# Moving three kinds of work between the even and the odd tiles of a 200-tile attention loop: value roundings, key parts, and the steps of a key part

## The chip, the cores and the metric

One core of one Trainium2 chip. The metric is device microseconds (us) of one execution of the whole program. Of the kernel before there are three timed runs and one execution that the hardware profiler recorded.

## What is computed

A layer norm, a cross attention with 16 heads of 32 channels, a residual, a second layer norm, a gated feed-forward block with quantised inputs and a second residual. 1600 query rows look at 5776 context rows. What the change touches lies in the attention: keys are quantised for each row and head, values for each channel over all rows.

```python
def _fq_sym(x, axis):
    s = jnp.max(jnp.abs(x), axis=axis, keepdims=True) / 127.0
    s = jnp.maximum(s, 1e-08)
    q = jnp.clip(jnp.round(x / s), -127.0, 127.0) * s
    return x + jax.lax.stop_gradient(q - x)
...
kv = (cond @ Wkv + bkv).reshape(1, -1, 2, H, hd)
k, v = (kv[:, :, 0], kv[:, :, 1])
...
q = _fq_sym(q, axis=-1)
k = _fq_sym(k, axis=-1)
v = _fq_sym(v, axis=2)
attn = jnp.einsum('bhqd,bhkd->bhqk', q, k)
attn = jax.nn.softmax(attn.astype(jnp.float32), axis=-1)
attn = _fq_unsigned(attn, axis=-1)
out = jnp.einsum('bhqk,bhkd->bhqd', attn, v)
```

## The kernel before

**Stages.** A prologue (up to about 140 us in the trace) makes the queries of all heads and the keys and values of heads 0 to 3. Then comes one loop of 200 tiles (140 to 1553 us), and last the feed-forward block.

**A tile** (the loop at L1231) is one head against one block of 128 query rows: 5776 scores for each row, made in five chunks. TensorE writes a chunk to PSUM (L1251; L1260 in a pair tile), and VectorE copies it to the buffer `score` while it takes the row maxima (L1267, called here an eviction). There are two score buffers, used in turn. GpSimd makes of the five maxima the bias of the exponential (L1299, then L1310 and L1311, the last called nb). ScalarE makes the exponentials as bytes in two halves (L1203): `pairc` at the end of the tile, `codes` in the tile after. SyncE issues a DMA transpose for each half (L1208, L1211), GpSimd unpacks the first half three tiles later (L1224), and TensorE multiplies with the values four tiles later (L1130).

**Groups.** Heads go in four groups of four, 50 tiles to a group. Tiles are numbered from 0 here, in the kernel 50 g + k; "tile 12" is k = 12 of a group, and even and odd are by that number. Two heads have 25 tiles: 13 for the first and 12 for the second, since tile 12 of the first is a pair tile: its 128 rows are the last 64 query rows of both heads, so it needs the keys of both.

**Side work.** While a group is scored, the keys and values of the next group are made, a pair of 126-row blocks in two tiles. TensorE projects (L276, L278) into one PSUM tile `pp` for each pair of blocks, of which there is a single buffer; ScalarE copies it out (`pair_keep`, L299, tile `vraw`) at the end of the odd tile, and only then TensorE goes on to the next pair in the even tile after. GpSimd rounds the keys (L316, L323, L324) in odd tiles.

**Key parts.** The keys of a head become a bf16 matrix kT in six parts. `keys_split` (L373) makes a sum of three bf16 pieces of a part on GpSimd: step 0 is L387 and L388, step 1 is L390 and L391, step 2 is L393. `keys_turn` (L395) transposes the pieces on TensorE (L400), `keys_keep` (L402) copies them to kT on ScalarE (L404). A pair (n, turn) in `PLAN["keys"]` or `LAST["keys"]` says: split from tile n on, turn and keep in tile `turn`. `plan_keys` (L730) puts steps 0 and 1 in tile n and step 2 in tile n + 1, or all three in tile n where turn is n + 1. The first of the four tuples is for the second head of the group itself; its last part is turned in tile 12.

**Values.** When all blocks of the next group are projected, `values_divide` (GpSimd, L360) and `values_round` (ScalarE, L363, to int8) go over the values in pieces that `PLAN["divide"]` lists, the first number being the tile, from tile 49 of one group to tile 15 of the next. They are planned by `plan_codes` (L747). Group 0 takes its own list, `CODES`, and the end of that of `PLAN["divide"]`; group 3 has a list of its own, `PLAN["end"]`. `values_copy` (L414, L419) makes the f16 values of one head in two halves, in the tiles that `PLAN["copy"]` names.

**Order.** Nothing is scheduled by a program: `put` (L727) adds a call to one of a tile's lists. In a tile, GpSimd does its list "pool", the unpacking, and then the maxima and nb. ScalarE does "act0" (kT copies) and `codes` of the tile before in the window that says "turn" in `WINDOWS` (L113), then "act" (the copy of `pp` first, then roundings), then its own `pairc`. Each engine takes its instructions in that order.

**Group 3** (`LAST`) makes no further keys and values. It runs the output projection instead (L790 to L807), with `part_turn` in every third tile from tile 8 on; if that tile turns no keys, four matmuls that are only there to keep TensorE busy (`keep_busy`, L817) are added.

Of the kernel before, what the change touches and what calls it, by code (L numbers as in the profile page):

```python
# [22 lines left out]
P = 128  # L23
C = 512
H = 16
HD = 32
# [3 lines left out]
NB = 46  # L30
# [18 lines left out]
MAXIMA = ((23, 0, 0, 24, 32), (35, 1, 24, 36, 64), (41, 2, 36, 42, 128))  # L49

CODES = (
    (1, 0, 4, 0, 128), (1, 4, 23, 0, 32), (1, 23, 46, 0, 32), (2, 4, 8, 32, 128), (3, 8, 24, 32, 64), (5, 24, 40, 32, 64),
)

PLAN = {

    "keys": (
        ((-4, 0), (2, 4), (4, 6), (6, 8), (8, 10), (10, 12)),
        ((12, 14), (14, 16), (16, 18), (18, 20), (20, 22), (22, 24)),
        ((24, 26), (26, 28), (28, 30), (30, 32), (32, 34), (34, 36)),  # L60
        ((36, 38), (38, 40), (40, 42), (42, 44), (44, 46), (48, 49)),
    ),
    "query": ((0, 4, 5), (14, 14, 18), (25, 27, 29), (39, 41, 43)),
    "copy": ((8, 10, 11), (19, 21, 23), (31, 33, 35), (50, 50, 51)),

    "max": (
        *((31 + i, 0, 0, 30, 16 * i, 16 * i + 16) for i in range(8)),
# [2 lines left out]
    "finish": (47, 48),  # L70

    "divide": (
        (49, 0, 23, 0, HD), (49, 23, NB, 0, HD), (50, 0, 4, HD, P), (51, 4, 8, HD, P), (51, 8, 24, HD, 2 * HD),
        (53, 24, 40, HD, 2 * HD), (55, 40, NB, HD, 2 * HD), (57, 8, 16, 2 * HD, P), (59, 16, 24, 2 * HD, P),
        (61, 24, 32, 2 * HD, P), (63, 32, 40, 2 * HD, P), (65, 40, NB, 2 * HD, P),
    ),
    "end": (
        (49, 0, 23, 0, HD), (49, 23, NB, 0, HD), (50, 0, 4, HD, P), (51, 4, 16, HD, P), (52, 16, 28, HD, P),
# [6 lines left out]

LAST = {
    "keys": (
        ((-4, 0), (4, 5), (6, 7), (8, 9), (10, 11), (11, 12)),
        tuple((n, n + 1) for n in range(12, 24, 2)),
        tuple((n, n + 1) for n in range(24, 36, 2)),  # L90
    ),
    "query": ((0, 4, 5), (14, 14, 18), (25, 27, 29)),
    "copy": ((8, 9, 10), (19, 21, 22), (31, 33, 34)),
# [52 lines left out]
def xattn_ffn(ctx: ExitStack, tc: tile.TileContext, xin, ctxt, wq, bq, wkv, bkv, wp, bp, w13, w2, nw, out):  # L146
# [340 lines left out]
    with (  # L487
# [165 lines left out]
        for t in range(NB):  # L653
# [11 lines left out]
            if t % 8 == 7 or t in (43, NB - 1):  # L665
                c0 = 44 if t == NB - 1 else t // 8 * 8
# [13 lines left out]
        for t in range(NT):  # L680
            n = WHEN["first"] + WHEN["every"] * t
# [13 lines left out]
        n = WHEN["first"] + WHEN["every"] * 7 + WHEN["store"] + 4  # L695
# [18 lines left out]
    with tc.manual_schedule():  # L714
# [12 lines left out]
        def put(n, where, fn, *args, first=False):  # L727
            plan[n][where].insert(0 if first else len(plan[n][where]), lambda: fn(*args))

        def plan_keys(h, n, turn, c0):  # L730
            if turn > n + 1:
                put(n, "pool", keys_split, h, c0, (0, 1))
                put(n + 1, "pool", keys_split, h, c0, (2,))
            else:
                put(n, "pool", keys_split, h, c0)
            put(turn, "turn", keys_turn, h, c0, psa)
            put(turn, "act0", keys_keep, h, c0)
# [282 lines left out]
        for g in range(H // G):  # L1020
            base = g * 50
            h = g * G
            own = LAST if g + 1 == H // G else PLAN
            for hx, starts in zip(range(h + 1, min(h + 5, H)), own["keys"]):
                for i, (n, turn) in enumerate(starts):
                    if base + n >= 0:
                        plan_keys(hx, base + n, base + turn, 8 * i)
            if g == 0:
                put(2, "act", query_load, h, 8 * P, NQ)

                for c, *fn in (
                    (0, warm_up, 5), (1, keys_turn, 0, 40, psa), (1, keys_keep, 0, 40), (1, values_max, 0, 3, 42, NB),
                    (2, values_turn, 0, 4, psa, "oacc"), (2, values_scale, 0), (2, values_diag, 0),
                    (2, keys_turn, 0, 44, psa), (2, keys_keep, 0, 44),
                    (4, values_spread, 0, psa, "oacc"), (4, values_keep, 0),
                ):
                    put(0, f"w{c}", *fn)
                for n in range(1, LAG):
                    for c in range(5):
                        put(n, f"w{c}", warm_up, 3 if c in (1, 3) else 1)  # L1040
                put(2, "w3", values_sum, 0, psa)
                put(2, "w3", values_sum_keep, 0, nc.scalar)
                put(2, "w4", values_rest, 0)
                put(3, "act0", values_rest_keep, 0, nc.scalar)
                for n, *args in (*CODES, *((n - 50, *args) for n, *args in PLAN["divide"] if n > 53)):
                    put(n, "pool", values_divide, 0, *args)
                    put(n, "act0" if args[0] == 0 else "act", values_round, 0, *args)
                put(2, "pool", values_copy, 0, 0)
                put(2, "pool", values_copy, 0, 1)
# [4 lines left out]
            if g + 1 == H // G:  # L1054
# [6 lines left out]
                for j in range(NT):  # L1061
                    n = base + LAST["first"] + 3 * j
# [13 lines left out]
                for k in range(8):  # L1076
                    n = base + LAST["piece"][k]
# [153 lines left out]
        for n in range(NTI):  # L1231
# [7 lines left out]
            h, t = tiles[n]  # L1239
# [190 lines left out]
```

## Time and profile before

| | |
|---|---|
| three timed runs | 1813.94, 1815.35, 1825.12 us; median 1815.35 us |
| the profiled execution | 1815.99 us |
| its span, first to last instruction | 1814.2 us |
| VectorE busy | 1692.9 us (93%) |
| TensorE matmul busy | 1624.5 us (90%) |
| ScalarE busy | 1485.2 us (82%) |
| GpSimd busy | 1322.3 us (73%) |
| TensorE clock granted, mean | 0.985 |

In the rows of the profile, engines are PE (TensorE), PEld (its weight loads), DVE (VectorE), ACT (ScalarE), POOL (GpSimd) and SP (SyncE); L360 is line 360 of the kernel before. A row of groups gives line, engine, operation, output<-input, shapes and count, then busy time and the mean of one, then the idle time before them and who ended it. A row of a timeline gives start and duration in us and, in brackets, the idle time before and who ended it.

### The profile page before, as it was taken

What the parts mean: (1) busy time and instruction counts of PE and PEld (TensorE: products, weight loads), DVE (VectorE), ACT (ScalarE), POOL (GpSimd) and SP (SyncE); (2) the same over time, 40 slices, a digit from 0 to 9 for tenths busy, and PEclk for the clock granted to TensorE, in tenths of its full rate; (3) what the DMA queues carried; (4) which work ended last, traced back from release to release, by engine and by line L of the source; (5) the groups of instructions that cost most, each with busy time, mean ns of one, the idle gap of its engine ahead of it and who ended that gap; (6) DMA issues with size and microseconds to landing.
All of it is one profiled execution on the core that took longest, in us unless ns stands there. A gap on an engine that the chain in (4) does not pass through costs nothing. (4 is left out here: it accounts for less than half of the span.)

```text
span 1814.2 us, 43710 instructions
## 1 busy us (share of the span) xinstructions
PE 1624.5 (90%) x16745; PEld 1139.5 (63%) x16745; DVE 1692.9 (93%) x2930; ACT 1485.2 (82%) x1471; POOL 1322.3 (73%) x1852
## 2 busy tenths in 40 slices
PE   7998989988898998888888988888998899889998
PEld 6985666656565665565566665655565555568886
DVE  7889999999999999999999999999899999788886
ACT  4557999988899998888999998998899988744443
POOL 5657989877899888788898887888777756542221
PEclk9999999999999999999999999999899999999999
DMA  5656999999999999999999999989999999821000
GB/s 169 158 146 131 208 209 204 207 202 212 189 208 204 210 209 207 206 210 194 199 204 205 208 221 207 201 157 201 196 215 208 211 210 238 185 81 36 30 27 21
DMA packets 982447, 323.87 MB, mean 179 GB/s; under 512 B 939943, under 2 KB 946267, under 8 KB 982238
## 3 DMA queue, kind: packets, MB, share of 16 engines
q1 hardware_dynamic: 970392, 300.91, 87.5%
q10 hardware_dynamic: 11846, 20.17, 3.9%
q8 instruction: 131, 2.15, 0.5%
q14 instruction: 78, 0.64, 0.1%
HBM read 79.16 MB, written 10.72 MB: 50 GB/s over the span
## 5 line engine op out<-in xcount | busy, mean ns | idle before, releaser
L1267 DVE TENSOR_SCALAR_CACHE_REDUCE score<-sl 128x1536 f32<-128x1536 f32 (+1 forms) x1000 | 1301.3, 1355 | 42.9 <-PE sl L1251 25.5
L1251 PE MATMUL sl<-kT,qT 96*128 96x512 bf16 (+1 forms) x2304 | 628.4, 367 | 117.3 <-DVE score L1267 107.4
L1203 ACT ACTIVATE pairc<-score,nb,qs 128x2772 uint8<-128x2772 f32 x192 | 518.4, 2700 | 73.2 <-POOL nb L1311 56.1
L1203 ACT ACTIVATE codes<-score,nb,qs 128x3024 uint8<-128x3024 f32 x192 | 558.2, 2907 | 19.3 <-DMA rT<-codes 18.0
L1224 POOL CAST rU<-pk 128x2816 f16<-128x2816 uint8 x200 | 506.4, 2532 | 6.5 <-DMA pk<-pairc 5.6
L276 PE MATMUL pp<-wkv,cb 128*128 128x256 f32 x1104 | 340.3, 389 | 22.4 <-ACT vraw L299 19.4
L1251 PEld LDWEIGHTS <-qT 96*128 96x128 bf16 x2304 | 184.0, 96 | 211.2 <-issue 140.7
L276 PEld LDWEIGHTS pp<-wkv,cb 128*128 128x128 f32 x1104 | 197.4, 190 | 122.4 <-ACT vraw L299 40.2
L1130 PEld LDWEIGHTS <-rT 128*128 128x128 f16 x4608 | 195.6, 96 | 94.9 <-issue 13.5
L1130 PE MATMUL oacc<-v,rT 128*128 128x32 f16 x4608 | 210.7, 177 | 4.8 <-ACT og L1169 3.5
L1310 POOL TENSOR_SCALAR m<-mx,m 128x1 f32<-128x1 f32 x200 | 72.5, 362 | 146.1 <-DVE score L1267 91.4
L1130 PEld LDWEIGHTS <-rU 128*128 128x128 f16 x4224 | 146.1, 96 | 42.6 <-issue 8.3
L1130 PE MATMUL oacc<-v,rU 128*128 128x32 f16 x4224 | 167.5, 177 | 0.0
L961 POOL TENSOR_TENSOR rw<-rl,nw_b 128x480 f32<-128x480 f32 (+3 forms) x39 | 49.1, 1260 | 151.4 <-DVE gq L991 63.6
L943 PE MATMUL p<-w13l,hT 128*128 128x480 f32 (+3 forms) x312 | 120.5, 386 | 3.8 <-POOL w13l L481 3.6
L943 PE MATMUL p<-w13h,hT 128*128 128x480 f32 (+3 forms) x312 | 122.3, 392 | 1.8 <-ACT hT L928 1.2
L404 ACT COPY kT<-kt 96x1008 bf16<-96x1008 bf16 (+2 forms) x97 | 90.7, 935 | 6.7 <-PE kt L400 6.5
L299 ACT COPY vraw<-pp 128x512 f32<-128x512 f32 x92 | 53.1, 578 | 45.9 <-DVE am L288 40.0
L1299 POOL TENSOR_SCALAR m<-mx 128x1 f32<-128x1 f32 x200 | 74.3, 372 | 18.2 <-DVE score L1267 18.1
L316 POOL TENSOR_TENSOR vraw<-vraw,rs 128x256 f32<-128x256 f32 x92 | 59.1, 643 | 35.8 <-DVE rs L311 22.8
L1267 DVE DVE_READ_ACCUMULATOR score<-sl 128x1 f32 x1000 | 83.3, 83 | 0.0
L943 PEld LDWEIGHTS p<-w13h,hT 128*128 128x128 f32 (+1 forms) x312 | 59.3, 190 | 16.9 <-ACT hT L928 7.0
(229 smaller groups left out, 2619.0 us busy)
## 6 DMA issues: line engine op xcount, KB each, us to landing
cb<-in SPq DMA_DIRECT2D x135, 256.0 KB
cr<-in SPq DMA_DIRECT2D x46, 256.0 KB
qT<-q_dram SPq DMA_DIRECT2D x45, 100.0 KB
pk<-pairc SPq DMA_TRANSPOSE x200
rT<-codes SPq DMA_TRANSPOSE x200
xn<-in ACTq DMA_DIRECT2D x12, 256.0 KB
x_s<-in ACTq DMA_DIRECT2D x12, 256.0 KB
x_dram<-x_s ACTq DMA_DIRECT2D x12, 256.0 KB
```

The lines of the kernel that those rows point to most:

```text
L276: nc.tensor.matmul(pp, cbs[g, t][:, kb, :], wts_g[g][:, kb, :], start=(kb == 0), stop=False)
L299: nc.scalar.copy(vraw.rearrange("p (u t) c -> p u t c", t=2)[:, u : k + 1 : k - u], pp.rearrange("p t (two c) -> p two t c", two=2),)
L316: nc.gpsimd.tensor_tensor(kv, kv, batch.pop(("rs", g, u)).unsqueeze(3).broadcast_to([P, 2, G, HD]), ALU.mult,)
L404: nc.scalar.copy(kT[h][:, c0 * KB : (c0 + n) * KB].rearrange("p (b k) -> p b k", k=KB), exp_.pop(("pt", h, c0))[:, :n, 2:])
L943: nc.tensor.matmul(pt[:r, :w], T["h", t][:, kb, :r], last_w[c][p][:, i * 4 + kb, :], start=(kb == 0 and p == 0), stop=(kb == 3 and p == 1),)
L1130: nc.tensor.matmul(oacc[h][:, t, :], turned(n, bl), v16[h][:, bl, :], start=(bl == turns[0]), stop=(bl == turns[-1]),)
L1203: nc.scalar.activation(dst, src, AF.Exp, bias=nb, scale=s1, accum_out=usum[:, i, n % 50 : n % 50 + 1])
L1224: nc.gpsimd.tensor_copy(r.rearrange("p (b two) q -> p b two q", two=2), packed.pop(n).bitcast(U8).rearrange("p b (q two) -> p b two q", tw ...
L1251: nc.tensor.matmul(sl[:, x0:x1], qT[h][:, t * P : (t + 1) * P], kT[h][:, col + x0 : col + x1], start=True, stop=True,)
L1267: nc.vector.tensor_scalar(sc[:, col : col + w], sl[:, :w], 1.0, None, ALU.mult, ALU.max, accum_out=mx[:, c : c + 1])
L1299: nc.gpsimd.tensor_scalar(m1, mx[:, 0:1], mx[:, 1:2], mx[:, 2:3], ALU.max, ALU.max)
L1310: nc.gpsimd.tensor_scalar(m2, mx[:, 3:4], mx[:, 4:5], m1, ALU.max, ALU.max)
```

## The change

The kernel's lists are edited, and one division of work.

- `plan_keys`: step 1 of a key part goes from tile n to tile n + 1, ahead of step 2, wherever the part is not turned in tile n + 1.
- `PLAN["divide"]`: all pieces from tile 51's second on move one tile later, so that from tile 52 to 66 they lie in even tiles, both the GpSimd division and the ScalarE rounding. `CODES` drops its last piece, and the filter for group 0 takes one entry more, so that the same pieces are done there one tile sooner or later than before.
- `PLAN["keys"]`, first tuple: parts two to six are split and turned two tiles sooner; the last turn is in tile 10. Group 0 keeps the old tiles (`FIRST_KEYS`).
- `PLAN["copy"]`: the two halves of the second head's values in tiles 7 and 9, not 8 and 10.
- `LAST["keys"]` (group 3): the second head's parts are turned in tiles 5, 6, 7, 9 and 10, not 5, 7, 9, 11 and 12; the parts of the third and fourth heads are placed at 0, 2, 3, 5, 6 and 8 tiles from tiles 12 and 24, not at every second tile. No key turn now shares a tile with a `part_turn`, so `keep_busy` adds its matmuls in five tiles more: 11, 17, 23, 29 and 35.

On VectorE and in SyncE's queue the order of instructions is the same; on GpSimd and ScalarE the same instructions stand in another order; TensorE gets 20 `keep_busy` matmuls more, and its key transposes stand elsewhere.

```diff
 CODES = (
-    (1, 0, 4, 0, 128), (1, 4, 23, 0, 32), (1, 23, 46, 0, 32), (2, 4, 8, 32, 128), (3, 8, 24, 32, 64), (5, 24, 40, 32, 64),
+    (1, 0, 4, 0, 128), (1, 4, 23, 0, 32), (1, 23, 46, 0, 32), (2, 4, 8, 32, 128), (3, 8, 24, 32, 64),
 )
+FIRST_KEYS = ((-4, 0), (2, 4), (4, 6), (6, 8), (8, 10), (10, 12))
...
     "keys": (
-        ((-4, 0), (2, 4), (4, 6), (6, 8), (8, 10), (10, 12)),
+        ((-4, 0), (1, 2), (2, 4), (4, 6), (6, 8), (8, 10)),
...
-    "copy": ((8, 10, 11), (19, 21, 23), (31, 33, 35), (50, 50, 51)),
+    "copy": ((7, 9, 11), (19, 21, 23), (31, 33, 35), (50, 50, 51)),
...
     "divide": (
-        (49, 0, 23, 0, HD), (49, 23, NB, 0, HD), (50, 0, 4, HD, P), (51, 4, 8, HD, P), (51, 8, 24, HD, 2 * HD),
-        (53, 24, 40, HD, 2 * HD), (55, 40, NB, HD, 2 * HD), (57, 8, 16, 2 * HD, P), (59, 16, 24, 2 * HD, P),
-        (61, 24, 32, 2 * HD, P), (63, 32, 40, 2 * HD, P), (65, 40, NB, 2 * HD, P),
+        (49, 0, 23, 0, HD), (49, 23, NB, 0, HD), (50, 0, 4, HD, P), (51, 4, 8, HD, P), (52, 8, 24, HD, 2 * HD),
+        (54, 24, 40, HD, 2 * HD), (56, 40, NB, HD, 2 * HD), (58, 8, 16, 2 * HD, P), (60, 16, 24, 2 * HD, P),
+        (62, 24, 32, 2 * HD, P), (64, 32, 40, 2 * HD, P), (66, 40, NB, 2 * HD, P),
     ),
...
 LAST = {
     "keys": (
-        ((-4, 0), (4, 5), (6, 7), (8, 9), (10, 11), (11, 12)),
-        tuple((n, n + 1) for n in range(12, 24, 2)),
-        tuple((n, n + 1) for n in range(24, 36, 2)),
+        ((-4, 0), (4, 5), (5, 6), (6, 7), (8, 9), (9, 10)),
+        *(tuple((n + i, n + i + 1) for i in (0, 2, 3, 5, 6, 8)) for n in (12, 24)),
     ),
...
             if turn > n + 1:
-                put(n, "pool", keys_split, h, c0, (0, 1))
-                put(n + 1, "pool", keys_split, h, c0, (2,))
+                put(n, "pool", keys_split, h, c0, (0,))
+                put(n + 1, "pool", keys_split, h, c0, (1, 2))
...
-                for i, (n, turn) in enumerate(starts):
+
+                for i, (n, turn) in enumerate(starts if g or hx > 1 else FIRST_KEYS):
...
-                for n, *args in (*CODES, *((n - 50, *args) for n, *args in PLAN["divide"] if n > 53)):
+                for n, *args in (*CODES, *((n - 50, *args) for n, *args in PLAN["divide"] if n > 52)):
```

## The prediction, on record before the changed kernel ran

> **What bounds the kernel now.** I read the page's engine shares first, then the costliest groups, then busy time by stretches of group 1, then the timeline of single tiles. The page:
>
> ```profile
> PE 1624.5 (90%) x16745; PEld 1139.5 (63%) x16745; DVE 1692.9 (93%) x2930; ACT 1485.2 (82%) x1471; POOL 1322.3 (73%) x1852
> ...
> L1267 DVE TENSOR_SCALAR_CACHE_REDUCE score<-sl 128x1536 f32<-128x1536 f32 (+1 forms) x1000 | 1301.3, 1355 | 42.9 <-PE sl L1251 25.5
> ```
>
> VectorE's evictions are the floor: only 42.9 us of idle time lie before them, so no reordering of side work can win more. Stretches of group 1 (us, then busy time of PE, PEld, DVE, ACT, POOL): two tiles without a stall, tiles 10 and 11, tile 12, tiles 18 to 33:
>
> ```profile
> 536.01:549.24 13.23, 12.15 (x146) 8.55 (x144) 13.23 (x23) 12.02 (x12) 12.19 (x19) 1.00 1.04 215
> ...
> 562.98:576.88 13.90, 12.77 (x158) 8.62 (x156) 13.37 (x23) 13.08 (x14) 12.86 (x20) 1.00 1.19 214
> 576.88:586.18 9.30, 7.37 (x83) 4.43 (x82) 6.84 (x13) 9.23 (x9) 8.40 (x13) 1.00 0.99 172
> ...
> 614.07:725.48 111.41, 100.24 (x1155) 68.22 (x1154) 108.66 (x181) 102.34 (x85) 95.27 (x145) 1.00 1.10 209
> ```
>
> A pair of tiles costs 13.23 when VectorE never waits; tile 12 costs 9.30 with 6.84 of VectorE work. Its stall in the timeline:
>
> ```profile
> 578.66 0.56 ACT L299 COPY vraw<-pp 128x512 f32<-128x512 f32 x1
> ...
> 580.94 1.76 DVE L1267 TENSOR_SCALAR_CACHE_REDUCE score<-sl 128x1536 f32<-128x1536 f32 x1 [1.15 <-PE sl L1260]
> ...
> 582.48 0.77 ACT L404 COPY kT<-kt 96x756 bf16<-96x756 bf16 x1
> ...
> 583.30 0.38 PE L1260 MATMUL sl<-kT,qT 96*64 96x512 bf16 x1 [0.82 <-ACT kT L404]
> 583.71 1.22 DVE L1267 TENSOR_SCALAR_CACHE_REDUCE score<-sl 128x1024 f32<-128x1024 f32 x1 [1.00 <-PE sl L1260]
> ```
>
> Two waits: 1.15 us because ScalarE copied `pp` late (TensorE may not project the next pair before, and the score matmuls queue behind that projection), and 1.00 us because the last key part reaches kT in the tile that uses it. Why the copy is late, on GpSimd:
>
> ```profile
> 552.71 0.67 POOL L390 TENSOR_TENSOR kd<-kd,stack 128x256 f32<-128x256 f32 x1
> 553.44 0.40 POOL L391 CAST stack<-kd 128x256 bf16<-128x256 f32 x1
> ...
> 558.36 0.26 POOL L1311 TENSOR_SCALAR nb<-m,nqs 128x1 f32<-128x1 f32 x1
> 558.70 1.27 POOL L360 TENSOR_TENSOR vraw<-vraw,tops 128x512 f32<-128x512 f32 x1
> 559.93 0.67 POOL L393 TENSOR_TENSOR stack<-kd,stack 128x256 bf16<-128x256 f32 x1
> ...
> 565.57 0.26 POOL L1311 TENSOR_SCALAR nb<-m,nqs 128x1 f32<-128x1 f32 x1
> ```
>
> GpSimd runs without a gap here. From one nb to the next an odd tile with a division takes 565.57 - 558.36 = 7.21, an even tile with steps 0 and 1 takes 6.42 (nb of tile 5 at 537.56, of tile 6 at 543.98). Last evictions end about 6.45 (odd) and 6.8 (even) after the ones before. So nb falls behind: it ends 0.90 after the last eviction where GpSimd keeps up, 2.07, 2.47, 3.11 and 3.14 after it in tiles 5, 7, 9 and 11. The exponentials wait for it, and the copy of `pp` behind `codes`. In tiles 7, 9 and 11 that copy ends 1.72, 1.82 and 2.34 into the next tile, and VectorE idles 0.42, 0.53 and 1.15; at 0.76 (tile 5) it doesn't. So it idles by what the copy ends beyond about 1.3.
>
> **The change part by part.**
>
> *Key part of tile 12, groups 1 and 2.* The wait of 1.00 goes in each: -2.0. The part is turned in tile 10; nothing reads it before tile 12. The five transposes, copies and splits that move two tiles sooner issue no DMA; SyncE's order is untouched. What is late next is the copy of `pp`, so no more than the 1.00 is counted.
>
> *Divisions and step 1 change places.* L390 and L391 take 1.23 with their gaps (525.30 to 526.53), the division of 128x512 also 1.23 (558.70 to 559.93). Where both exist, the GpSimd passes stay 6.42 and 7.21. But the second key part is now split whole in tile 1: the three steps take 2.77 busy (0.63, 0.40, 0.67, 0.40, 0.67), some 3.0 with gaps, and a division of 1.27 leaves for tile 2. So nb of tile 1 ends at about 0.9 + 1.3 = 2.2, not 0.91; the value copy (0.80) in tiles 7 and 9 makes these passes 8.0; tiles 10 and 11 shrink to some 5.3.
>
> *Roundings in even tiles.* On ScalarE, odd `pairc` to even `pairc` takes 6.48 now (524.09 to 530.57, with the kT copy), even to odd 6.1 and a rounding of 0.6. After: 7.1 and 6.1. Queued behind the rounding are the tile's own `pairc`, then `codes` and the copy of `pp`, for which TensorE waits; before, the rounding stood behind that copy. The copy ends 0.7 less into the next tile than the even `pairc` starts after its last eviction (tile 4: 1.46 and 0.76). Carried on from tile 1, `pairc` starts 2.1, 2.2, 2.9, 2.8 and 2.65 late in tiles 2, 4, 6, 8 and 10, stalls in between included. VectorE then idles 0.6, 0.2, 1.0, 0.8 and 1.0 in tiles 4, 6, 8, 10 and 12, and as before 0.67 in tile 2: 4.3. Before it was 0.67, 0.11, 0.42, 0.53 and, of tile 12, 1.46 without the kT wait: 3.2. So +1.1 each in groups 1 and 2: +2.2. Bounds: -1.5 if the fuller ScalarE only loses the gaps that it has now (0.83, 0.59 and 0.54 before `pairc` in tiles 5, 8 and 9), +4 if each of six roundings delays TensorE by its 0.61.
>
> *Group 0.* The kT wait stays. By the same steps (tile 3's pass grows by 1.23, tile 4's rounding comes before the copy) idle time goes from 3.7 to 4.3: +0.6, bounds -1 and +2.5.
>
> *Step 1 in odd tiles outside the divisions.* The odd pass grows from 7.21 - 1.23 = 5.98 to 7.21, the even one falls to 5.19. Odd nb ends at 0.9 + 7.21 - 6.45 = 1.7; the even pass makes that good. `pairc` of the even tile then starts 1.7 + 6.48 - 6.8 = 1.4 late, and the copy of `pp` ends at 0.7, inside the 1.3: nothing, covered by 0.6 us of slack. Tiles 19 and 21 also make value copies (0.80): `pairc` 2.2 late, copy at 1.5, idle 0.15 each. In tiles 31 to 41 the maxima (L330) stretch tiles to 7.4 and more, which hides it. With a DMA wait now and then I take +0.25 for each of three groups: +0.8. Bounds: 0, and +5 (21 odd tiles by 0.24).
>
> *Group 3.* Tiles 11 and 12 idle 0.91 and 3.41 us, tiles 35 to 37 together 2.0. Both follow a drop of TensorE's clock, the columns being as above with the clock third from the right (tile 12, then tile 35 and the one after):
>
> ```profile
> 1287.42:1297.60 10.18, 10.18 (x92) 5.66 (x93) 6.77 (x10) 8.05 (x7) 6.79 (x11) 0.61 0.88 191
> 1447.30:1454.60 7.30, 5.17 (x55) 3.40 (x54) 6.47 (x11) 6.74 (x6) 3.96 (x7) 0.84 1.08 168
> 1454.60:1462.30 7.70, 7.70 (x76) 4.47 (x76) 6.85 (x11) 5.68 (x4) 2.96 (x3) 0.71 1.17 268
> ```
>
> Tiles 11 and 35 are two of those that now get four busy matmuls (0.38 each, 1.5 us of work) in TensorE's pauses of about 1.0, and no key transposes. If the clock holds there, all 6.3 can go. Against it: three key parts now follow in tiles 4, 5 and 6, and two in 8 and 9. A whole split is some 3.0 on GpSimd, beside weight scalings of 1.59 (L780) in tiles 6 and 8, so nb ends up to 4 late, and `codes` of tiles 8 and 9 may hold VectorE for 1 to 1.5 in tiles 10 and 11. I take -4.0 (most of the clock stalls, less 1.5, less what stays); bounds -6.3 and +2. The first is the nearer, since the clock rows show those stalls themselves.
>
> The Trainium skill, "TensorE: Matmul & The Clock Gate", section "What's actually happening", says that the clock falls to half after an idle window of some 3.4 us. That rule speaks against this gain: no pause of that length precedes these drops in the rows, only pauses of about 1.0 (TensorE was busy 5.17 of 7.30 us). By the rule the fillers would change nothing and this term would be the key part alone, about -1.0, and the sum +0.6, 1816.0. I go by the rows.
>
> **Sum.** -2.0 + 2.2 + 0.6 + 0.8 - 4.0 = -2.4. The profiled execution took 1815.99 (span 1814.2), 0.64 over the median of the three runs (1815.35). On that median: 1813.0.
>
> **The rivals.**
>
> *GpSimd becomes the bound of odd tiles* (slower). Place: tiles 13 to 29 and 43 to 47 of groups 0 to 2, some 30 odd tiles without a division. It decides once nb ends over 2.35 late there, 0.65 more than worked out; then each such tile can cost 0.6: +18, 1833. For it: POOL is gapless in the divided tiles already. Against: the even pass of 5.19 leaves 1.6 us free.
>
> *Roundings hold up TensorE more than carried above* (slower). 0.61 in each of seven even tiles of three groups: +13, less the 2.0: 1826. For it: the copy of `pp` now stands behind the rounding. Against: in tile 12 ScalarE catches up.
>
> *The change doesn't do what it says.* In tile 12 the copy of `pp` stands in front anyway, and clock drops come elsewhere in group 3: all terms but +1 vanish, 1816. For it: the 1.15 wait comes first in tile 12.
>
> *Faster.* ScalarE's gaps close, group 3 gives its 6.3, and stalls that follow late transposes (tile 20 of group 2 idles 2.68, tiles 27 and 28 1.3) do not return: -2 - 3 - 6.3 + 0.6 - 4 = -14.7: 1801. Against: these have the same DMA order after.
>
> **How the numbers follow.** Chances: forecast 0.50, not what it says 0.20, faster rival 0.12, roundings 0.13, GpSimd bound 0.05. The range 1803 to 1824 leaves out the last, half of the roundings and some of the faster rival. About 1%, 18 us, is what a measurement of this kernel can tell from no change: faster by over 1% is 0.03 (beyond the faster rival's whole price), slower 0.05 (the GpSimd rival), within 0.92. The likeliest case's own range is 1808 to 1818.
>
> **What would show it.** Right: no kT wait in tile 12 of groups 1 and 2, its idle time near 1.0; odd nb some 0.8 later outside the divisions, without idle time before evictions; full clock in tiles 12 and 35 of group 3. Wrong: idle time before evictions well over or under 40 us in all, with TensorE waiting for L299 in even tiles from 14 on, or clock drops where fillers now stand.

## The result and the profile after

| | before | after |
|---|---|---|
| median of 20 runs each | 1816.63 us (1809.88 to 1830.48) | 1824.60 us (1818.21 to 1833.22) |
| the profiled execution (span) | 1815.99 us (1814.2) | 1822.92 us (1821.1) |
| its loop of 200 tiles | 1412.8 us | 1419.6 us |
| VectorE's idle time in the loop | 43.3 us | 49.7 us |
| mean granted TensorE clock | 0.985 | 0.985 |

The ratio of after to before is 1.0038, with a 95% interval of 1.0023 to 1.0053: the change costs about 7 us. The forecast was 1813.0 us. All of it lies in the loop (+6.8 us; before and behind the loop +0.8 and -0.6), and of that 6.4 us is VectorE's idle time. By group of 50 tiles the loop grows by 0.4, 2.0, 1.4 and 3.0 us. In the kernel after, most lines of the scoring loop have a number higher by one (the evictions are L1268, `pairc` is L1204, nb is L1312).

The page of after, engine shares and the row of the evictions:

```profile
PE 1631.5 (90%) x16785; PEld 1147.7 (63%) x16785; DVE 1692.6 (93%) x2930; ACT 1483.1 (81%) x1471; POOL 1323.5 (73%) x1852
...
L1268 DVE TENSOR_SCALAR_CACHE_REDUCE score<-sl 128x1536 f32<-128x1536 f32 (+1 forms) x1000 | 1301.3, 1355 | 49.3 <-PE sl L1252 34.1 <-PE sl L1261 9.1 <-issue 2.0
```

VectorE does the same work in the same time (1301.3 us); what grows is the idle time before it, 42.9 to 49.3 us. Busy time by stretches of after, in the columns of the prediction: a tile without any trouble but the carried lateness (tile 4 of group 1), tile 12 of group 1, then tiles 10, 35 and 36 of group 3.

```profile
523.60:530.82 7.22, 6.10 (x76) 4.26 (x75) 6.72 (x10) 6.95 (x8) 6.88 (x10) 1.00 0.91 182
579.04:589.57 10.53, 9.37 (x78) 5.18 (x77) 7.11 (x12) 8.35 (x8) 6.29 (x10) 0.68 0.96 170
1277.65:1293.40 15.75, 9.45 (x99) 5.92 (x98) 7.04 (x12) 10.77 (x12) 8.79 (x10) 0.78 0.94 152
1456.88:1463.60 6.72, 5.80 (x58) 4.02 (x57) 6.72 (x11) 6.06 (x5) 3.66 (x5) 1.00 0.95 186
1463.60:1470.14 6.54, 5.74 (x68) 3.56 (x66) 6.31 (x10) 5.60 (x4) 3.52 (x4) 1.00 1.16 257
```

Tiles 35 and 36 are repaired: full clock, 6.72 and 6.54 us where they took 7.30 and 7.70. Tile 12 of group 1 got longer (10.53, it was 9.30), at a granted clock of 0.68. And tile 10 of group 3 takes 15.75 us, more than two tiles; before it took 7.02, with VectorE busy throughout:

```profile
1273.00:1280.02 7.02, 6.71 (x93) 4.19 (x92) 7.01 (x11) 6.99 (x7) 6.30 (x10) 1.00 1.16 225
```

**Where the idle time went**, from the VectorE rows of both traces, tile by tile (us in the loop):

| tiles | before | after | difference |
|---|---|---|---|
| group 3, tile 10 | 0.00 | 8.48 | +8.48 |
| group 3, tiles 11 and 12 | 4.32 | 0.35 | -3.97 |
| group 3, tiles 31 to 37 | 2.23 | 0.82 | -1.41 |
| groups 1 and 2, tile 12 | 4.64 | 7.29 | +2.65 |
| groups 1 and 2, tiles 1 to 11 | 3.83 | 5.41 | +1.58 |
| group 0, tiles 1 to 12 | 5.28 | 5.93 | +0.65 |
| all others | 23.0 | 21.4 | -1.6 |

**Tile 10 of group 3**, timeline of after:

```profile
1278.61 2.91 ACT L1204 ACTIVATE codes<-score,nb,qs 128x3024 uint8<-128x3024 f32 x1
...
1278.86 0.50 PE L400 MATMUL kt<-ident_b,stack 128*96 128x128 bf16 x6
...
1282.11 2.70 ACT L1204 ACTIVATE pairc<-score,nb,qs 128x2772 uint8<-128x2772 f32 x1 [0.50 <-POOL nb L1312]
...
1284.80 0.77 ACT L404 COPY kT<-kt 96x756 bf16<-96x756 bf16 x1
...
1285.62 0.81 PE L425 MATMUL vs<-v,pick 128*12 128x64 f16 x12 [6.26 <-ACT kT L404]
...
1286.60 1.44 PE L1252 MATMUL sl<-kT,qT 96*128 96x512 bf16 x3
...
1288.17 1.76 DVE L1268 TENSOR_SCALAR_CACHE_REDUCE score<-sl 128x1536 f32<-128x1536 f32 x1 [7.37 <-PE sl L1252]
```

Read it from TensorE's wait of 6.26 us. The matmuls of L425 (`values_sum`, the sums of a head's values) write a PSUM tile that has one buffer (tag "tr"), and the transposes of a key part (L400) write the same one. In group 3 the sum stands in the last tile that `LAST["copy"]` names, tile 10; the last key part was turned in tile 12 and is now turned in tile 10. So the sum must wait until ScalarE has copied the part out (L404), and that copy stands in ScalarE's queue behind `codes` (2.91) and `pairc` (2.70). TensorE takes its instructions in order: the score matmuls behind L425 wait too, and VectorE idles 7.37 us. The clock halves in this pause, from 1284.4 us for 6.8 us, and most of the tile's other 1.1 us of idle time falls into that half clock.

**Tile 12 of groups 1 and 2**, timeline of after:

```profile
580.74 0.56 ACT L299 COPY vraw<-pp 128x512 f32<-128x512 f32 x1
...
581.35 1.22 PE L276 MATMUL pp<-wkv,cb 128*128 128x256 f32 x2 [1.16 <-ACT vraw L299]
...
582.58 1.49 PE L1261 MATMUL sl<-kT,qT 96*64 96x512 bf16 x6
...
584.21 1.76 DVE L1268 TENSOR_SCALAR_CACHE_REDUCE score<-sl 128x1536 f32<-128x1536 f32 x1 [2.02 <-PE sl L1261]
...
586.79 1.23 DVE L1268 TENSOR_SCALAR_CACHE_REDUCE score<-sl 128x1024 f32<-128x1024 f32 x1 [0.82 <-PE sl L1261]
```

The kT wait is gone, as forecast, and the copy of `pp` comes as late as forecast. But from 581.2 us on TensorE has half its clock for 6.8 us: the projection takes 1.22 instead of 0.70 us and the six score matmuls 1.49 instead of 0.84. The tile idles 3.65 us instead of the 1.0 foretold.

**GpSimd.** One row of the waits of after, then the same row of before (us in total, times, longest):

```profile
ACT pairc L1204 <- POOL nb L1312: 86.9, 94, 4.2
```

```profile
ACT pairc L1203 <- POOL nb L1311: 62.0, 71, 3.1
```

ScalarE waits 25 us longer for nb. In group 1, `pairc` starts 2.04, 1.99, 2.76, 2.56 and 2.31 us late in tiles 2, 4, 6, 8 and 10 (forecast 2.1, 2.2, 2.9, 2.8, 2.65), and VectorE idles 0.68, 0.50, 0, 0.85 and 0.66 there (forecast for tiles 2 to 10: 0.67, 0.6, 0.2, 1.0, 0.8).

### The profile page after: what moved, and what is told of

The parts are those of the page before. It is cut to its first block, busy times and chain, and to the rows that moved or that the text cites. A ratio compares the mean times of both kernels' runs of the same rounds, so it can differ in the third digit from the quotient of the medians.

```text
span 1821.1 us, 43791 instructions
## 1 busy us (share of the span) xinstructions
PE 1631.5 (90%) x16785; PEld 1147.7 (63%) x16785; DVE 1692.6 (93%) x2930; ACT 1483.1 (81%) x1471; POOL 1323.5 (73%) x1852
## 5 line engine op out<-in xcount | busy, mean ns | idle before, releaser
L1268 DVE TENSOR_SCALAR_CACHE_REDUCE score<-sl 128x1536 f32<-128x1536 f32 (+1 forms) x1000 | 1301.3, 1355 | 49.3 <-PE sl L1252 34.1
L1204 ACT ACTIVATE pairc<-score,nb,qs 128x2772 uint8<-128x2772 f32 x192 | 518.4, 2700 | 93.2 <-POOL nb L1312 78.6
L1204 ACT ACTIVATE codes<-score,nb,qs 128x3024 uint8<-128x3024 f32 x192 | 558.0, 2906 | 9.2 <-DMA rT<-codes 6.8
L404 ACT COPY kT<-kt 96x1008 bf16<-96x1008 bf16 (+2 forms) x97 | 90.6, 934 | 7.1 <-PE kt L400 6.9
L1268 DVE DVE_READ_ACCUMULATOR score<-sl 128x1 f32 x1000 | 83.0, 83 | 0.0
```

What stands on the lines that cost most here:

```text
L404: nc.scalar.copy(kT[h][:, c0 * KB : (c0 + n) * KB].rearrange("p (b k) -> p b k", k=KB), exp_.pop(("pt", h, c0))[:, :n, 2:])
L1204: nc.scalar.activation(dst, src, AF.Exp, bias=nb, scale=s1, accum_out=usum[:, i, n % 50 : n % 50 + 1])
L1268: nc.vector.tensor_scalar(sc[:, col : col + w], sl[:, :w], 1.0, None, ALU.mult, ALU.max, accum_out=mx[:, c : c + 1])
```

## The experiments

All ratios are to the kernel before, run on the same chip in the same rounds, with 95% intervals; 0.1% is 1.8 us. The expectations number the theories: theory 1 is the shared PSUM tile of group 3; theory 4 says that the roundings cost because they now stand ahead of the copy of `pp`; theory 5 says that it is the fuller odd pass of GpSimd that costs. Diffs are shown cut to the lines that matter.

### Is it the shared PSUM tile?

**e1_sum12**: the kernel after, with the sum of group 3 moved out of the tile of the key turn.

```diff
-    "copy": ((8, 9, 10), (19, 21, 22), (31, 33, 34)),
+    "copy": ((8, 9, 12), (19, 21, 22), (31, 33, 34)),
```

> The changed kernel with one number edited: in group 3 the sum of the second head's values (values_sum) moves from tile 10, where the last key part is now turned too, to tile 12. Theory 1 (both use the one PSUM tile named tr, and TensorE waits there until ScalarE has copied the key part out behind an exponential): the 6.3 us wait of L425 for L404 goes, idle time of VectorE in tile 10 of group 3 falls from 8.5 to under 1.5, and the time from 1824.6 to about 1817. Rival (GpSimd is late after three key parts in tiles 4 to 6 and two in 8 and 9, and the exponentials hold VectorE): idle time of tile 10 stays over 5, the time within 2 of the changed kernel's.

Measured: 1817.26 us, ratio 1.0010 (0.9989 to 1.0032). After had 1.0038, so this one number is worth about 0.28% of the 0.38%, give or take 0.26%. Tile 10 of group 3 in its timeline:

```profile
1276.71 0.98 ACT L404 COPY kT<-kt 96x1008 bf16<-96x1008 bf16 x1
...
1280.62 1.76 DVE L1268 TENSOR_SCALAR_CACHE_REDUCE score<-sl 128x1536 f32<-128x1536 f32 x1 [0.80 <-ACT codes L1204]
...
1283.78 0.76 ACT L404 COPY kT<-kt 96x756 bf16<-96x756 bf16 x1
```

The last part is still copied out late (1283.78), and nobody waits for it: the tile idles 0.80 us instead of 8.48. Its profiled execution was one of its slowest (1825.4 us) for other reasons: the clock was at half for 10.2 us around tile 48 of group 3 and tiles 41 to 49 idled 9.2 us, where after idled 2.1 with the same instructions there, and group 0 idled 12.8 us (after 9.1), its tile 12 alone 2.2 us more, with a drop of the clock.

**e2_sum11_before**: the converse in the kernel before, which turns a key part in tile 11.

```diff
-    "copy": ((8, 9, 10), (19, 21, 22), (31, 33, 34)),
+    "copy": ((8, 9, 11), (19, 21, 22), (31, 33, 34)),
```

> The kernel before with one number edited: in group 3 values_sum moves from tile 10 to tile 11, where that kernel turns a key part. Nothing else moves, so GpSimd is no later. Theory 1 (one PSUM tile for both): TensorE waits for the key copy at L425 for 4 us or more in tile 11, VectorE idles some 5 more there, the time rises by 4 to 7. Rival: no new wait, the time stays within 1 of the kernel before.

Measured: 1821.26 us, ratio 1.0026 (0.9999 to 1.0053). Its timeline of tile 11:

```profile
1283.58 0.97 ACT L404 COPY kT<-kt 96x1008 bf16<-96x1008 bf16 x1
1284.60 0.80 PE L425 MATMUL vs<-v,pick 128*12 128x64 f16 x12 [5.17 <-ACT kT L404]
...
1287.43 1.22 DVE L1267 TENSOR_SCALAR_CACHE_REDUCE score<-sl 128x1024 f32<-128x1024 f32 x1 [5.89 <-PE oacc L1130]
```

The same pair of steps in one tile makes the same stall in another kernel and another tile: 5.17 us of TensorE, 6.18 us of VectorE in tile 11 (0.91 before). (The last row names the matmuls that TensorE did just before those that VectorE waits for.) By the traces theory 1 is shown from both sides. Part of the stall is given back, tile 12 idling 0.14 instead of 3.41, and the time's interval just reaches no difference.

**e4_last_only** and **e5_last_sum12**: the kernel before with the new `LAST["keys"]` alone, then with the sum in tile 12 as well.

```diff
 LAST = {
     "keys": (
-        ((-4, 0), (4, 5), (6, 7), (8, 9), (10, 11), (11, 12)),
-        tuple((n, n + 1) for n in range(12, 24, 2)),
-        tuple((n, n + 1) for n in range(24, 36, 2)),
+        ((-4, 0), (4, 5), (5, 6), (6, 7), (8, 9), (9, 10)),
+        *(tuple((n + i, n + i + 1) for i in (0, 2, 3, 5, 6, 8)) for n in (12, 24)),
     ),
...
-    "copy": ((8, 9, 10), (19, 21, 22), (31, 33, 34)),
+    "copy": ((8, 9, 12), (19, 21, 22), (31, 33, 34)),
```

> The kernel before with the changed keys of group 3 alone. Theory: this is the larger half of the loss: tile 10 of group 3 idles about 8.5, tiles 11 and 12 together under 0.5 where the kernel before has 4.3, tiles 35 to 37 about 0.6 where it has 2.0; the sum is +2 to +4 us. The forecast on record had -4 for this part.

> The kernel before with the changed keys of group 3 and the sum of values in tile 12, nothing else. Theory 1 (the collision in tile 10 ate what the new places give): idle time of tiles 8 to 13 of group 3 falls from 4.9 to about 1.5 and that of tiles 31 to 38 from 2.2 to 0.8, the time by 4 to 5 under the kernel before. Rival (clock drops come at random and the places are worth nothing): within 1 of the kernel before.

Measured: e4 1820.58 us, 1.0015 (0.9996 to 1.0034); e5 1816.56 us, 0.9992 (0.9972 to 1.0011). In e4 tile 10 of group 3 idles 5.66 us, TensorE waiting 3.7 for the copy to kT; in e5 it idles 0.75. In both, tiles 11 and 12 idle 0.35 and 1.04 where before idled 4.32, and tiles 31 to 37 idle 0.82 where it idled 2.23. So the gains that the forecast put into group 3 are there, and the collision turns them into a loss. They are not as large in every execution: of the six profiles with the old places the clock halves in tile 35 in four (before, e2, e9, e10; not in e8 and e11, where tiles 31 to 37 idle 0.83), of the eight with the new places in none. Of the gain of 4 to 5 us that was expected of e5, its middle value shows 1.5, within an interval that reaches from -5 to +2: that it is a gain is not shown. What its runs do show is a higher clock: granted 0.9894 on average over 12 runs, 0.9867 over the 35 of before beside them.

### Tile 12 and the clock

**e3_warm12**: the kernel after, with six matmuls whose result nobody reads in TensorE's pause in tile 12 of groups 1 and 2.

```diff
+        def warm_pair(h):
+            busy = psa.tile([P, C], F32, name="warm", tag="tr")
+            for _ in range(6):
+                nc.tensor.matmul(busy, ident_b[0 : 3 * HD, :], kT[h][:, 0:C], start=True, stop=True)
...
+            if g:
+                put(base + 12, "w1", warm_pair, h)
```

> The changed kernel with six matmuls of 96x512 more, about 1.3 us of TensorE work, in tile 12 of groups 1 and 2, ahead of the projection that waits for the copy of pp. Theory 2 (TensorE's clock halves in tile 12 because the key transposes left it and TensorE pauses): the clock stays at 1.00 there, idle time of VectorE falls from 3.65 to about 1.2 in each, the time by about 4.5 from 1824.6. Rival (the late copy alone holds VectorE): idle time stays at 3.5 or rises by the added work.

Measured: 1824.77 us, ratio 1.0041 (1.0020 to 1.0061). The place did what was expected. Its timeline of tile 12 of group 1:

```profile
580.93 1.47 PE L833 MATMUL warm<-kT,ident_b 96*128 96x512 bf16 x6
...
582.85 0.84 PE L1268 MATMUL sl<-kT,qT 96*64 96x512 bf16 x6
...
583.82 1.76 DVE L1275 TENSOR_SCALAR_CACHE_REDUCE score<-sl 128x1536 f32<-128x1536 f32 x1 [0.83 <-PE sl L1268]
```

Full clock, 1.08 and 1.09 us of idle time in the two tiles. But the median is that of after: the 4.5 us that was expected did not come. One reason is in e1, which has the same code as after in these tiles and no filler: it idles 1.05 and 0.51 us there, at full clock. The drop is not in every execution, and the filler repairs only those that have it. Against e1, which differs from e3 by the filler and the sum alone, e3 is 7.5 us slower: that is the collision again, with whatever the fillers themselves cost.

### Which part costs in groups 0 to 2

**e9_split_only** (the edit of `plan_keys` alone), **e10_rounds_only** (`PLAN["divide"]`, `CODES` and the filter for group 0 alone), **e8_split_rounds** (both), **e11_keys_only** (first tuple of `PLAN["keys"]`, `FIRST_KEYS` and the first entry of `PLAN["copy"]` alone): each is the kernel before with these lines of the change's diff.

```diff
-                put(n, "pool", keys_split, h, c0, (0, 1))
-                put(n + 1, "pool", keys_split, h, c0, (2,))
+                put(n, "pool", keys_split, h, c0, (0,))
+                put(n + 1, "pool", keys_split, h, c0, (1, 2))
```

> The kernel before with step 1 of a key part in the later tile, alone. GpSimd's odd pass with a division grows from 7.2 to about 8.4. Theory 5 (the fuller odd pass is what costs, by idle time in tiles 4 to 12 and by odd nb elsewhere): 2 to 3 over the kernel before. Rival (it costs only together with the moved roundings): within 1.

> The kernel before with the divisions and roundings in even tiles, alone. GpSimd's even pass with a division grows to about 7.65, the odd one falls to 5.98. Theory 5: within 1.5 of the kernel before, since GpSimd's longest pass stays near what it was. Rival (theory 4, roundings ahead of the copy of pp cost by themselves): 2 or more over it.

> The kernel before with step 1 in the later tile and the roundings and divisions in even tiles, no key part moved. Theory 4: 2 to 4 over the kernel before, with idle time of 2.9 in tiles 4 to 8 of group 0 and TensorE waiting for L299 in even tiles. Rival (these two parts only change places, and cost nothing): within 1 of it.

> The kernel before with the second head's key parts two tiles sooner and its value copies one tile sooner in groups 1 and 2, alone. Tile 12 there idles 1.1 where no clock drop falls in it, not 2.5, and tiles 4 to 10 idle 0.5 to 1.5 more: within 2 of the kernel before, either way. If idle time of tile 12 is 3.7 in this profile too, a clock drop fell in it again.

| | median | before beside it | ratio (95%) | wait of `pairc` for nb |
|---|---|---|---|---|
| e9: split | 1823.79 | 1817.67 | 1.0036 (1.0019 to 1.0052) | 81.5 us |
| e10: roundings and divisions | 1816.89 | 1817.67 | 0.9991 (0.9975 to 1.0006) | 63.8 us |
| e8: both | 1821.47 | 1819.18 | 1.0016 (0.9998 to 1.0034) | 75.4 us |
| e11: keys | 1821.93 | 1817.67 | 1.0029 (1.0008 to 1.0050) | 67.7 us |

The row of the waits in e9, against the 62.0 of before:

```profile
ACT pairc L1203 <- POOL nb L1311: 81.5, 90, 3.2
```

Moving the roundings ahead of the copy of `pp` costs nothing that these runs can tell from zero: theory 4 falls. The median of e8 lies where theory 4 put it, 2 to 4 us over before, but e8 has the split too, and the split costs that much alone (e9). With the divisions left in the odd tiles, their GpSimd pass gets longer: nb ends 2.87, 2.83, 2.94, 3.56 and 3.58 us late in tiles 3, 5, 7, 9 and 11 of group 1 (1.68, 2.07, 2.47, 3.11 and 3.14 before), and tile 12 idles 2.90. Theory 5 holds for the lateness. For the price only in part: the idle time of groups 0 to 2 grows by 3.3 us in e9's profile, against a median 6.1 us higher; the rest of its longer profile lies in group 3, whose instructions e9 doesn't change, with drops of the clock at other places.

The keys alone cost because the second part is then split in tile 1, where the division of tile 51 still stands: nb of tile 1 ends 3.52 us late (0.91 before), and tile 4 idles 2.36 us with a drop of the clock. Tile 4 of group 1 in e11 (the same columns as above):

```profile
521.72:530.95 9.23, 7.40 (x76) 4.82 (x75) 7.09 (x13) 9.01 (x9) 8.59 (x13) 0.82 1.06 210
```

After takes 7.22 for this tile, since its division has left tile 1: nb of tile 1 ends 2.32 late there, and tile 4 idles 0.50. So in the traces moving the divisions makes room that the keys need. In the times this is not shown: 0.36 for the split, -0.09 for the divisions, 0.29 for the keys and 0.15 for `LAST` (e4) are 0.71%, and the whole change costs 0.38%, but with intervals of 0.15 to 0.21 on each of the five the difference of 0.33 can be noise.

**e7_keys_last** (e5 with the keys of e11) and **e6_rounds_back** (e7 with the new split; it is e1 with the divisions and roundings in their old tiles):

> The same and the second head's key parts and value copies two and one tiles sooner in groups 1 and 2. Theory 3 (the kT wait in tile 12 is real, 1.0 in each group, and GpSimd's added lateness in tiles 1 to 9 gives about half back): 0 to 2 under the last kernel, tile 12 of groups 1 and 2 idle 1.0 to 1.5 where it has 2.5. Rival (the copy of pp holds tile 12 anyway): idle time of tile 12 stays over 2.

> The same and step 1 of a key part in the later tile; this is the changed kernel with the sum in tile 12 and the roundings and divisions in odd tiles as before. GpSimd's odd pass with a division grows to about 8.4, the even one falls to 5.2. Theory 4 (the roundings in even tiles are what costs in groups 0 to 2, as they stand ahead of the copy of pp): idle time of tiles 4 to 8 of group 0 falls from 2.9 to under 1.5, the time is 2 to 4 under the kernel with everything (1817.3). Rival (GpSimd's odd pass is what costs): it is equal to it or above, as the odd pass is now 1.2 longer.

Measured: e7 1819.71 us, 1.0002 (0.9982 to 1.0022); e6 1821.43 us, 1.0014 (0.9999 to 1.0029). Putting the roundings back behind the copy of `pp` (e6) does not help against e1 (1.0010): theory 4 falls here as well; tiles 4 to 8 of group 0 idle 2.3 us in e6, not under 1.5 (2.9 in after). e7's tile 12 of groups 1 and 2 idles 3.71 and 3.75 us with drops of the clock, e6's 1.09 and 1.09 without.

### A version that keeps what worked

**e12_turn11**: e5 with the last part turned in tile 11, whole, in place of the new tiles of the second head's parts.

```diff
-        ((-4, 0), (2, 4), (4, 6), (6, 8), (8, 10), (10, 12)),
+        ((-4, 0), (2, 4), (4, 6), (6, 8), (8, 10), (10, 11)),
...
-    "copy": ((8, 10, 11), (19, 21, 23), (31, 33, 35), (50, 50, 51)),
+    "copy": ((8, 10, 12), (19, 21, 23), (31, 33, 35), (50, 50, 51)),
```

> A version meant to beat both kernels: the kernel before with the changed keys of group 3 and its sum in tile 12, and in groups 0 to 2 the second head's last part alone turned one tile sooner, in tile 11, its sum of values moved from there to tile 12 so that the two don't share a tile. Theory: the kT wait of 1.0 in tile 12 goes in three groups, the copy of pp in tile 11 stands 0.8 later behind the kT copy and gives most of it back; with group 3's gain 3 to 5 under the kernel before. If the copy gives all back, 1.5 to 2 under it, as without this step.

Measured: ratio 0.9979 (0.9958 to 0.9999), but the medians are equal (1817.99 beside 1817.67). The step that was meant did not do its work; timeline of tile 12 of group 1:

```profile
586.25 1.49 PE L1259 MATMUL sl<-kT,qT 96*64 96x512 bf16 x6
587.88 1.76 DVE L1266 TENSOR_SCALAR_CACHE_REDUCE score<-sl 128x1536 f32<-128x1536 f32 x1 [3.34 <-PE sl L1259]
```

The whole split in tile 10 makes nb and the copy of `pp` later still (that copy ends 3.34 us into tile 12; 2.34 before), and the clock drops as well: 4.80 us of idle time in this tile. If e12 is faster, it is by what it has of e5. No kernel here is shown to beat the kernel before by more than a few microseconds, and this interval only just excludes no difference.

## Why the prediction was wrong

Forecast -2.4 us with a range up to 1824; measured +6.9 us by the ratio, with a median of 1824.60, just above that range. "Within 1%" was right, the sign wrong. By its own steps:

- **Group 3, -4.0: the step that failed.** Measured +3.4 us of idle time in the profile (+3.0 of duration), past the bound of +2. What it named came: the clock holds in tiles 35 and 36, and tiles 11 and 12 lose 3.97 us, 31 to 37 lose 1.41. Its "against it" asked what three key parts in a row do to GpSimd, nb and `codes`. It didn't ask what else a turned part uses: a PSUM tile with one buffer, which the sum of the values in tile 10 takes too. That wait makes tile 10 idle 8.48 us, against 0.80 without it (e1), and e2 makes it anew in the kernel before. A smaller slip: four fillers are eight records of 0.38 us, 2.2 us of work in tile 35 of after, not 1.5.
- **kT wait of tile 12, -2.0: right as a wait, wrong as time.** The wait is gone everywhere. The idle time foretold (1.0) stands in executions without a drop of the clock (1.05 in e1, 1.09 in e6); with a drop it is 3.6 to 3.8, more than the 2.46 and 2.18 of before. Kernels that turn the part before tile 12 and have no filler there (after, e1, e6, e7, e11, e12) show drops in 7 of their 12 profiled tiles of groups 1 and 2; those that turn it in tile 12 (before, e2, e4, e5, e8, e9, e10) in 1 of 14. Transposes in the tile are no guarantee: in group 0 all but e12 turn the part in tile 12, and three of these 13 tiles have a drop (e1, e3, e9). Without e12, the ten tiles idle 2.3 us on average: over executions, the term is about nothing. All runs of e11, the keys alone, say the same of the clock: granted 0.9827 on average over 12 runs, 0.9862 over the 35 of before beside them; at 0.75 us for each 0.001 (last section, this chip) I estimate that as 2.7 us of the 4 that e11 costs. Where in the tiles that clock is lost, the means can't say. What the prediction missed is that the transposes which it moved away filled part of the stretch ahead of TensorE's pause there (66% busy with them, 62% without; last section); in e3's profile matmuls in the pause hold the clock. It saw that role for the fillers of group 3 and not here.
- **Roundings in even tiles, +2.2: right in the lateness, about half in size, and not by the roundings.** In tiles 2 to 10 of group 1 the lateness of `pairc` is within 0.35 us of the forecast. Idle time there was forecast to go from 1.7 to 3.3 us in each group and goes from 1.62 and 2.22 to 2.69 and 2.72. (The 0.11 for tile 4 before is that of group 0; in group 1 it is 0.) The roundings and divisions alone (e10) leave it at 2.02 and 2.01, the keys alone (e11) make it 3.33 and 3.34. So the cost seems to come with the part split whole in tile 1, from which the forecast carried the lateness on; no run has that split without the other moved keys.
- **Group 0, +0.6: the sum right, partly by luck.** Tiles 1 to 12 change by +0.65. But the 3.7 that the forecast started from is tiles 4 to 12, and these go to 5.5, not 4.3: tile 6 idles 2.17 where it idled 0, with a drop of the clock. Tile 2, which the forecast left out, gives back 1.21.
- **Step 1 outside the divisions, +0.8: right in the lateness.** Odd nb ends 1.2 to 1.6 late there (forecast 1.7), 2.4 in the copy tiles 19 and 21; in groups 0 and 1 the tiles behind these idle 0 and 0.2. Idle time of tiles 13 to 30 changed by +0.5, -0.8 and -0.9 in groups 0 to 2, so no cost can be seen in this profile; that e9, which has this and the fuller odd pass of tiles 3 to 11, costs 0.36% leaves it open.
- **The rivals.** "GpSimd becomes the bound" would need nb over 2.35 late in plain odd tiles: in groups 0 to 2 it is 1.6 at most, 2.3 in tile 43 and 2.4 in the copy tiles 19 and 21. "Roundings hold up TensorE" gave 1826, near the time, by a mechanism that e10 excludes (-0.09%, at most +0.06%). "Doesn't do what it says" and "faster" both took the stalls of group 3 as gone or kept, not doubled.
- **The rule of the Trainium skill** that the prediction set against the rows ("TensorE: Matmul & The Clock Gate", section "What's actually happening", half clock after an idle window) would have put group 3 at -1.0. The rows were the better guide there, since the fillers and the new tiles did hold the clock in tiles 35 and 36, and in tile 35 of all eight profiles that have them.

What stays open: how the 3.3 us between e5 and e1 (ratios 0.9992 and 1.0010) divides among the tiles of groups 0 to 2, since intervals of 0.2% are wider than that; and what e3's fillers are worth over many executions.

## What to carry to other kernels

Before a step is moved into another tile, list all that it uses besides its engine, the single-buffered PSUM tile above all, and who else has that buffer in the new tile and who frees it: two users in one tile cost a whole turn of the freeing engine's queue (6.26 us here). Matmuls or transposes in a pause may be what keeps TensorE's clock up; moving them away can cost more than the wait that they caused (3.65 us of idle time in tile 12 with a drop of the clock, 2.46 before). Try the parts of a change alone and in pairs, since one can make the room that another needs (nb of tile 1 is 3.52 us late with the keys alone, 2.32 in after, where the divisions moved too).

## What the runs showed of the hardware

**The clock changes on a fixed grid of 3.413 us, whose phase differs from execution to execution.** In each of the 14 profiled executions all drops in the loop begin at one and the same remainder modulo 3413.33 ns, to 3 ns, and last 3.4, 6.8 or 10.2 us; the remainder is another one in each execution. I laid this grid over each loop and took TensorE's matmul busy share in every cell at full clock: 5652 cells, 92 of them followed by half clock. Of the 34 cells up to 0.525 busy, 33 were followed by half clock; around 0.55 20 of 29, around 0.60 15 of 79, around 0.65 7 of 124, around 0.70 8 of 258, around 0.75 2 of 242, and above that 7 of 4886. A cell at half clock is followed by full clock mostly when TensorE was busy throughout it (87 of the 92 returns). So a drop needs no idle stretch; a cell that is little more than half busy is often enough. The busy share is not the whole rule, as the cells around 0.60 show.

The 3.4 us ahead of the end of the copy of `pp` in tile 12 of group 1 (each stretch ends 0.1 us before it), in after (clock then halves), e1 (it doesn't), e3 and before:

```profile
577.80:581.20 3.40, 2.11 (x35) 1.10 (x31) 3.40 (x8) 3.40 (x4) 1.93 (x5) 1.00 1.05 207
```

```profile
581.45:584.85 3.40, 2.12 (x36) 1.12 (x32) 3.40 (x8) 3.40 (x5) 1.92 (x5) 1.00 1.06 224
```

```profile
578.60:582.00 3.40, 3.11 (x41) 1.62 (x37) 3.40 (x8) 3.40 (x4) 1.94 (x5) 1.00 1.02 205
```

```profile
575.72:579.12 3.40, 2.25 (x32) 1.24 (x31) 3.40 (x8) 3.40 (x4) 3.30 (x4) 1.00 1.17 223
```

After and e1 are equally busy there (2.11 and 2.12 of 3.40, 62%). In after one cell of the grid, 577.82 to 581.24, takes in nearly the whole pause and is 0.61 busy; in e1 two cells meet near the start of the pause, at 583.71, and are 0.92 and 0.67 busy. With the transposes (before) the stretch is 66% busy, with the fillers (e3) 91%. In all 14 profiles, tile 12 of groups 0 to 2: where the 3.413 us up to the end of the copy are at most 0.605 busy (14 tiles), 9 have a drop; where they are 0.629 or more (28 tiles), 3 have. That the grid's phase is what parts after from e1 is an inference from these rows; no run could set the phase.

The Trainium skill, "TensorE: Matmul & The Clock Gate", section "What's actually happening", gives a free-running window of 3413 ns that makes the moment of a change vary by run, and this agrees with the grid. It gives "after ≥1 idle window" for the fall to half clock, and this doesn't agree: most cells ahead of the drops are half to two thirds busy and two of the 92 are idle throughout, and the longest pause in the one above is 1.16 us.

**It goes with the spread of the times.** Among the 35 runs of the kernel before on each of three chips, 0.001 of mean granted clock goes with 0.75 to 1.0 us (correlation -0.70 to -0.73), and the runs spread by 16 to 20 us. One profiled execution can thus show or lack several microseconds of stalls that the same instructions have in another; sums of idle time over tiles of a single profile are to be read with that in mind.
